# Row counts of direct transfers in a two-layer graph kernel: 128, 32 and 10 rows become 67 and 61, 17 to 31, and 17

## The chip, the cores and the metric

The kernel runs on one core of a Trainium2 chip. The metric is the device time of one execution in microseconds (us). The core has five engines with a queue of instructions each: TensorE (PE; its weight loads are shown as PEld), VectorE (DVE), ScalarE (ACT), GpSimd (POOL) and SyncE (SP). SyncE and ScalarE start direct transfers here, GpSimd starts the gathers, and 16 DMA engines move the bytes of all of them. The names of a queue in the profile end in q where an instruction only starts a transfer (SPq, ACTq, POOLq).

## The reference

Two message-passing layers over a graph with N = 6,250 nodes and E = 200,000 edges, sorted by their target node. A node has 160 numbers: 64 scalars and 32 vectors of three.

```python
# layer one: messages from the source node's row and 4 edge numbers (e0 and the vector e1)
out0 = C0 * (ss * e0 @ W1 + dot * INV3 @ W2)          # ss, vv: rows x[src]
out1 = C1 * (p3 + p4 + p5)                             # products of ss, vv, e0, e1 with W3, W4, W5
m_agg = segment_sum(concat(out0, out1), dst)           # then Ws, Wv, relu, + x
x = layernorm(x + layer_one)
# layer two: weights of the message from 10 edge features
h = relu(edge_length_embedded @ W_fc1 / sqrt(10)) * sqrt(2)
w = h @ W_fc2 / sqrt(100)                              # 192 weights per edge
y = linear(x)[src]
m0, m1, m2, m3 = products of w, y and the 4 edge numbers
out = si(x) + 0.5 * linear(segment_sum(m0..m3, dst))
x = layernorm(x + out)
```

## The kernel before

**Chunks.** The edges are cut into 391 chunks of 512 (128 partitions by J = 4). A written-out order (`ORDER`) mixes the first 312 chunks with the last 79; the last ones have two windows of target nodes each. For every chunk four gathers (`gathered`, L206) fetch the 512 source rows of 640 bytes, from `x` in layer one (`layer = 0` in the code) and from the table `ytab` in layer two. The gathered rows go into a ring of `GRING = 8` chunks.

**Steps.** `sums(layer, ...)` writes one step after another. In step t the chunk at place t of the order is loaded, that of place t - 1 gets its one-hot matrix (`onehot`, VectorE) and in layer two its hidden weights (`hidden`, TensorE L394, in pairs of chunks), place t - 2 its messages (`message`, TensorE L407 and VectorE L410 and L415), place t - 3 its sums on TensorE (`matmuls`, L427), and place t - 4 is added to the running sums (`add`, VectorE). In layer one, where no message is computed, the lags are 0, 1, 2 and 3. Each engine executes its own instructions in the order in which they are written.

**Blocks.** When the last chunk of a block of 128 target nodes is done (`CLOSE[b]`; 49 blocks, the last of 106 rows), the block's own stages follow at fixed lags. In layer one: the node rows are fetched 4 steps after the close (`fetch`, L486), used at lag 8 (`residual`), and the results go to `ytab` and `btab` at lag 14 (`written`, L533 on ScalarE's queue, L537 on SyncE's). In layer two: `btab` is fetched at lag 3 (L486), used at lag 6 (`residual_last`), and the output block is normalized on VectorE and sent at lag 8 (`sent`, L559). Blocks of low node numbers are long: in steps 66 to 200 one closes every 8 steps or so, after that one about every 4.

**The transfers on SyncE's queue.** Besides node rows there are two kinds. Edge attributes (4 numbers per edge, 2,048 bytes per chunk and quarter) come for 32 chunks at a time in four transfers of up to 32 rows into the tile `raw` (L368), asked for 8 steps ahead, and VectorE turns them (L374). Edge features (10 numbers per edge, layer two) come for four chunks at a time, in two transfers of 10 rows with two pieces of 2,048 bytes each (L342; single chunks at the end, L346). They go by turns into the tiles `et` and `early`, are written in the step of their first chunk, and TensorE uses them from the next step on. SyncE executes all of these in the order written, so a transfer that waits for its source or for its tile holds up those behind it.

Of the kernel before, what the change touches and what calls it, by code (L numbers as in the profile page):

```python
# [10 lines left out]
F32 = mybir.dt.float32  # L11
# [7 lines left out]
P = 128  # L19
# [4 lines left out]
J = 4  # L24
CH = P * J
NCH = -(-E // CH)
# [14 lines left out]
HALF = 312  # L41
NWIN = HALF + 2 * (NCH - HALF)
WIDTHS = ((3, 32), (128, 16), (208, 24), (HALF, 32), (NCH, 24))
GRING = 8
PREPARE = 8


def expected(node, sign):
# [30 lines left out]
POS = {c: i for i, c in enumerate(ORDER)}  # L79
# [13 lines left out]
CLOSE = closings()  # L93


def floor_of(c):

    done = [b for b in range(NB) if CLOSE[b] < POS[c]]
    near = [b for b in done if (b >= LATE) == (c >= HALF)] or [b for b in done if b < LATE]
    return P * (max(near) + 1) if near else 0  # L100


def windows(c):
# [108 lines left out]
def windowed(ctx: ExitStack, tc: tile.TileContext, x, srcs, rel, low, ident, iota, early, ahead, ea, sh, avec,  # L212
# [6 lines left out]
    nc = tc.nc  # L219
    const = ctx.enter_context(tc.tile_pool(name="const", bufs=1))  # L220
    dram = ctx.enter_context(tc.tile_pool(name="dram", bufs=1, space=bass.MemoryType.DRAM))
    ytab = dram.tile([N, D], F32, name="ytab")
    btab = dram.tile([N, D], F32, name="btab")

    acc = const.tile([P, 5, NW], F32, name="acc")
    bank = ctx.enter_context(tc.tile_pool(name="bank", bufs=1, space=PSUM)).tile([P, 512], F32, name="bank")
# [13 lines left out]
    def clear(k):  # L240
        nc.scalar.activation(acc[:, k, :], zero[:, 0:1].to_broadcast([P, NW]), AF.Copy)  # L241
# [70 lines left out]
    def sums(layer, table, gp, hp):  # L312
        with ExitStack() as s:
# [11 lines left out]
            G, S, SH, ET, H, M, PA, AT, RAW = {}, {}, {}, {}, {}, {}, {}, {}, {}  # L325

            def load(c):
                if layer or c not in ahead:
                    G[c] = gathered(nc, gp.tile([P, J, D], F32, name="g"), srcs, table, c)
                else:  # L330
                    G[c] = ahead.pop(c)
                if c % 4 == 0 and layer:

                    if POS[c] % 8 >= 4:
                        et = xp.tile([P, 2, CH], F32, name="et")
                    else:
                        et = early.rearrange("p a j d -> p (a j d)")
                        et = et[:, :2 * CH].rearrange("p (s e) -> p s e", s=2)
                    ET[c // 4] = et
                    for i in range(2):  # L340
                        if c + 4 <= NCH:
                            nc.sync.dma_start(et[64 * i:64 * i + 10, :, :],  # L342
                                              ea[:, c * CH:(c + 4) * CH].rearrange("f (s i e) -> f s i e", s=2, i=2)[:, :, i, :])
                        else:
                            for k in range(c + i, NCH, 2):
                                nc.sync.dma_start(et[64 * i:64 * i + 10, (k - c) // 2, :], ea[:, k * CH:(k + 1) * CH])  # L346
# [12 lines left out]
            def group(c):  # L359
                return c - (c - (c >= HALF) * HALF) % 32  # L360

            def attributes(first, n):

                raw = RAW[first] = hp.tile([P, 512], F32, name="raw")
                if n < 32:
                    nc.vector.memset(raw, 0.0)
                for q in range(4):
                    nc.sync.dma_start(raw[32 * q:32 * q + n, :],  # L368
                                      sh[first:first + n, 32 * q:32 * q + 32, :].rearrange("c p f -> c (p f)"))
# [4 lines left out]
                nc.vector.transpose(sht, RAW.pop(first).rearrange("r (p f) -> r f p", f=16))  # L374

            def onehot(c):
                if group(c) == c:
# [6 lines left out]
                attr = SH[group(c)][:, :, c - group(c)].rearrange("p (j k) -> p j k", j=J)  # L384
# [98 lines left out]

            def rows_of(name, table, b):
                t = T[name, b] = np_.tile([P, D], F32, name=name)
                nc.sync.dma_start(t[:rows(b)], table[b * P:b * P + rows(b), :])  # L486

            def fetch(b):
                rows_of("xt", x, b)
# [50 lines left out]
            def fetch_base(b):  # L540
# [15 lines left out]

            def sent(b):
                normed("o", b)
                nc.sync.dma_start(out[b * P:b * P + rows(b), :], T.pop(("o", b))[:rows(b)])  # L559
# [8 lines left out]
            for t in range(max(CLOSE.values()) + 16):  # L568
                for f, lag in stages:
                    if 0 <= t - lag < NCH:  # L570
                        f(ORDER[t - lag])
                for f, lag in reversed(parts):
                    for b in range(NB):
                        if CLOSE[b] == t - lag:
                            f(b)
                if not layer:
                    for k in range(2 * t, min(2 * t + 2, 5)):
                        clear(k)
                if not layer and t == PREPARE:
                    prepare(up, pn)  # L580

# [392 lines left out]
```

## Time and profile before

| | |
|---|---|
| median of 10 runs | 3979.72 us (3978.03 to 3981.49) |
| the profiled execution | 3980.59 us, of which the span from first to last instruction is 3978.4 us |
| TensorE busy, mean granted clock | 3245.4 us (82%), 0.784 |
| VectorE busy | 2189.7 us (55%) |
| GpSimd busy | 2964.8 us (75%) |
| ScalarE busy | 380.5 us (10%) |
| moved by DMA | 295.60 MB, 74 GB/s on average |
| handover from layer one to layer two | GpSimd idle from 1978.3 to 2000.6 us |

A busy share says how much of the span an engine was executing; it is an average over two layers with different loads. The waits say what ended an idle stretch. A group of instructions is named by its line, its engine and output<-inputs. A row of the windows has the stretch, its length, then the busy time and (x) the instructions of TensorE, its weight loads, VectorE, ScalarE and GpSimd, then TensorE's granted clock as a share of full speed, the share of DMA time, and GB/s. A row of the timeline has the start, the duration, the engine, the line, the operation, output<-input, the count, and in brackets the idle time before it and what ended it. The queue rows give packets, megabytes, and the time that the packets took as a share of 16 engines' span.

### The profile page before, as it was taken

The page shows a single profiled execution, that of the slowest core. Times are in us where ns is not written, and L with a number is a line of the kernel's source. Part 1 is how long each engine was busy: PE and PEld are TensorE (multiplying, and loading weights), DVE is VectorE, ACT ScalarE, POOL GpSimd, SP SyncE. Part 2 cuts the span into 40 slices and gives each one's busy share as a digit, 9 for nine tenths or more (in the row PEclk, how much of TensorE's full clock was granted, in tenths as well). Part 3 has the DMA queues.
Part 4 walks back from the last instruction along what each step waited for, and adds up shares of the span by engine and source line. Part 5 has one row for each costly group of instructions (what it writes and reads, how often), then busy time and mean ns, then how long its engine had stood idle before and what let it go on. Part 6 is the DMA issues. An engine that isn't in the chain of part 4 may idle for free.

```text
span 3978.4 us, 42324 instructions
## 1 busy us (share of the span) xinstructions
PE 3245.4 (82%) x12714; PEld 2142.5 (54%) x12715; DVE 2189.7 (55%) x6948; ACT 380.5 (10%) x747; POOL 2964.8 (75%) x3137
## 2 busy tenths in 40 slices
PE   2777777777777777777788998998999999999998
PEld 2444444444444444455555665665666666666665
DVE  4222323233333333344457677777777778788887
ACT  2000000000000000000111111111111111111111
POOL 6777777777777777777667777777777777777775
PEclk8555555565555656666689999999999999999999
DMA  2222222222222222222222222222222222222222
GB/s 76 70 69 66 71 73 68 74 71 75 74 76 73 76 71 78 74 80 79 75 69 73 70 76 73 75 74 74 76 80 76 77 77 77 75 79 77 80 77 67
DMA packets 198245, 295.60 MB, mean 74 GB/s; under 512 B 59270, under 2 KB 140668, under 8 KB 198010
## 3 DMA queue, kind: packets, MB, share of 16 engines
q0 software_dynamic: 150144, 256.45, 24.3%
q1 hardware_dynamic: 40702, 31.55, 2.6%
q10 hardware_dynamic: 7164, 4.80, 0.4%
q8 instruction: 107, 1.75, 0.2%
q14 instruction: 128, 1.05, 0.1%
HBM read 280.57 MB, written 12.00 MB: 74 GB/s over the span
## 4 chain that ended last, share of the span: by engine, by line
POOL 28%; issue 22%; DMA 21%; PE 17%; DVE 11%; ACT 1%; DVEq 0%; POOLq 0%; SPq 0%; ACTq 0%
POOL g L206 28%; DMA g<-in_x,srcs 13%; PE ab L427 10%; DMA g<-ytab,srcs 8%; DVE m L415 3%; PE ph L461 2%; DVE m L410 2%; PE pw L407 2%; DVE S L385 2%; DVE ab L445 1%; DVE ab L444 1%; PE ph L394 1%; PE pl L526 1%; ACT acc L241 1%; DVE bank L381 1%
## 5 line engine op out<-in xcount | busy, mean ns | idle before, releaser
L206 POOL DMA_INDIRECT g<-ytab,srcs x1564 | 1480.0, 946 | 498.5 <-issue 397.9
L206 POOL DMA_INDIRECT g<-in_x,srcs x1556 | 1472.5, 946 | 475.2 <-issue 390.5
L427 PE MATMUL ab<-g,S 128*128 128x160 f32 (+1 forms) x3744 | 1183.5, 495 | 520.6 <-DMA g<-in_x,srcs 405.1
L427 PEld LDWEIGHTS ab<-g,S 128*128 128x128 f32 (+1 forms) x3744 | 727.2, 287 | 984.8 <-DMA g<-in_x,srcs 694.1
L427 PE MATMUL ab<-m,S 128*128 128x320 f32 (+1 forms) x3760 | 966.0, 445 | 14.6 <-DVE acc L449 14.3
L407 PE MATMUL pw<-fc,h 100*128 100x192 f32 x3128 | 660.2, 343 | 145.7 <-DVE m L415 73.3
L427 PEld LDWEIGHTS ab<-m,S 128*128 128x128 f32 (+1 forms) x3760 | 613.8, 193 | 235.3 <-issue 55.5
L447 DVE STREAM_TRANSPOSE ab<-ab 128x160 f32<-128x160 f32 x470 | 170.9, 364 | 1012.9 <-PE ab L427 1012.0
L407 PEld LDWEIGHTS pw<-fc,h 100*128 100x128 f32 x3128 | 501.9, 190 | 414.9 <-issue 298.4
L410 DVE TENSOR_TENSOR m<-pw,g 128x256 f32<-128x256 f32 x782 | 329.3, 421 | 366.1 <-DMA g<-ytab,srcs 313.3
L415 DVE TENSOR_TENSOR m<-g,pw 128x192 f32<-128x192 f32 x1564 | 475.6, 345 | 0.0
L385 DVE TENSOR_TENSOR S<-bank,sh 128x384 f32<-128x384 f32 (+2 forms) x782 | 431.4, 552 | 59.3 <-PE ab L427 9.6
L397 ACT ACTIVATE h<-ph 100x512 f32<-100x512 f32 x391 | 233.4, 597 | 1636.5 <-PE ph L394 1443.1
L449 DVE TENSOR_TENSOR acc<-acc,ab 128x120 f32 (+2 forms) x940 | 261.7, 278 | 186.5 <-PE ph L461 129.6
L381 DVE TENSOR_TENSOR bank<-iota,rel 128x96 f32<-128x96 f32 (+2 forms) x782 | 199.5, 255 | 19.2 <-PE bank L548 18.9
L445 DVE STREAM_TRANSPOSE ab<-ab 32x160 f32<-32x160 f32 x470 | 165.5, 352 | 16.2
L444 DVE STREAM_TRANSPOSE ab<-ab 128x160 f32<-128x160 f32 x470 | 167.4, 356 | 11.1 <-issue 8.2
L461 PE MATMUL ph<-wb,acc 128*128 128x160 f32 (+1 forms) x490 | 135.9, 460 | 0.1
L461 PEld LDWEIGHTS ph<-wb,acc 128*128 128x128 f32 (+1 forms) x490 | 127.9, 325 | 9.1 <-issue 8.7
L394 PE MATMUL ph<-early,fc 10*100 10x512 f32 x392 | 111.8, 633 | 2.2 <-DMA early<-in_ea 2.2
L394 PE MATMUL ph<-et,fc 10*100 10x512 f32 x390 | 109.0, 627 | 2.6 <-DMA et<-in_ea 2.6
L497 ACT ACTIVATE rl<-ph 128x160 f32<-128x160 f32 (+1 forms) x49 | 14.9, 304 | 833.6 <-PE ph L461 833.6
(80 smaller groups left out, 796.9 us busy)
## 6 DMA issues: line engine op xcount, KB each, us to landing
g<-ytab,srcs POOLq DMA_INDIRECT x1564
g<-in_x,srcs POOLq DMA_INDIRECT x1556
raw<-in_sh SPq DMA_DIRECT2D x88, 64.0 KB
early<-in_ea SPq DMA_DIRECT2D x98, 40.0 KB
xt<-in_x SPq DMA_DIRECT2D x48, 80.0 KB
ytab<-y ACTq DMA_DIRECT2D x48, 80.0 KB
btab<-base SPq DMA_DIRECT2D x48, 80.0 KB
et<-in_ea SPq DMA_DIRECT2D x96, 40.0 KB
```

Source lines behind the costliest of these rows:

```text
L206: nc.gpsimd.indirect_dma_start(out=g[:, j, :], out_offset=None, in_=table, in_offset=bass.IndirectOffsetOnAxis(ap=srcs[:, c, j:j + 1], axi ...
L381: nc.vector.tensor_tensor(oh[:, :, :w], iota[:, None, :w].to_broadcast([P, J, w]), rel[:, c, :, None].to_broadcast([P, J, w]), op=ALU.is_e ...
L385: nc.vector.tensor_tensor(S[c][:, :, :, :w], oh[:, :, None, :w].to_broadcast([P, J, 4, w]), attr[:, :, :, None].to_broadcast([P, J, 4, w]) ...
L394: nc.tensor.matmul(ph[:, i, :], fc1[g:g + 10, :], ET[c // 4][g:g + 10, c % 4 // 2, :], start=True, stop=True)
L397: nc.scalar.activation(H[c], H["p"][:, c % 2, :].rearrange("f (p j) -> f j p", j=J), AF.Relu, scale=FC_SCALE)
L407: nc.tensor.matmul(pw[:, j, :], h[:, q + j, :], fc2, start=True, stop=True)
L410: nc.vector.tensor_tensor(mq[:, :, :, 0:64], pw[:, :, 0:128].rearrange("p j (a u) -> p j a u", a=2), y[:, :, None, 0:64].to_broadcast([P, ...
L415: nc.vector.tensor_tensor(mq[:, :, a, 64:160].rearrange("p j (d u) -> p j d u", d=3), y1, pw[:, :, None, w:w + 32].to_broadcast([P, 2, 3, ...
L427: nc.tensor.matmul(ab[:, :n], one[h * i:h * i + h, j, :, :], t[h * i:h * i + h, j, :], start=(j == 0), stop=(j == J - 1), skip_group_check ...
L444: nc.vector.transpose(tr, blocks[:, 1])
L449: nc.vector.tensor_tensor(v, v, tr[:, :, :width(c)], op=ALU.add)
L461: nc.tensor.matmul(po[:r], lhs, weights[:, g, :], start=(g == 0), stop=(g == 4))
```

## The change

Every direct transfer of the running layers is given another row count. The bytes that are computed with stay the same.

- Attributes: the groups of 32 chunks become 15 groups of 31, 23, 19 or 17 chunks (`SIZES`). `group` now returns first chunk and size. The tile is cleared on VectorE before every group; before, only where a group had fewer than 32 chunks.
- Node rows: `fetch`, `fetch_base`, `written` and `sent` go through `sent_rows`, which makes two transfers of 67 and 61 rows out of one of 128. Blocks that close in the last 8 steps, and the block of 106 rows, keep one transfer.
- Edge features: in layer one, at steps 32, 64, ... 256, an eighth of the 10 feature rows is copied into a new table of 17 rows in device memory (`etab`), in one transfer of 10 rows and one that fills rows 10 to 16 with copies of rows 0 to 6. In layer two 17 rows are loaded from it where 10 were loaded from the input. TensorE still reads the first 10.

```diff
+LEADS = 67
+ROWS = 17
+SIZES = (31, 31, 31, 31, 31, 31, 23, 23, 23, 19, 19, 19, 31, 31, 17)
+COPIES = 8
...
+def group(c):
+
+    first = 0
+    for n in SIZES:
+        if c < first + n:
+            return first, n
+        first += n
...
+    etab = dram.tile([ROWS, NCH * CH], F32, name="etab")
...
-                            nc.sync.dma_start(et[64 * i:64 * i + 10, :, :],
-                                              ea[:, c * CH:(c + 4) * CH].rearrange("f (s i e) -> f s i e", s=2, i=2)[:, :, i, :])
+                            nc.sync.dma_start(et[64 * i:64 * i + ROWS, :, :],
+                                              etab[:, c * CH:(c + 4) * CH].rearrange("f (s i e) -> f s i e", s=2, i=2)[:, :, i, :])
...
-            GROUPS = sorted(((a, min(32, end - a)) for begin, end in ((0, HALF), (HALF, NCH))
-                             for a in range(begin, end, 32)), key=lambda g: POS[g[0]])
+            GROUPS = sorted({group(c) for c in range(NCH)}, key=lambda g: POS[g[0]])
...
-                if n < 32:
-                    nc.vector.memset(raw, 0.0)
+                nc.vector.memset(raw, 0.0)
...
+            def sent_rows(engine, b, to, from_):
+
+                cut = LEADS if CLOSE[b] < NCH - 8 and rows(b) == P else rows(b)
+                for part in (slice(0, cut), slice(cut, rows(b))):
+                    if part.start < part.stop:
+                        engine.dma_start(to[part], from_[part])
...
-                nc.sync.dma_start(t[:rows(b)], table[b * P:b * P + rows(b), :])
+                sent_rows(nc.sync, b, t, table[b * P:b * P + rows(b), :])
...
-                nc.scalar.dma_start(ytab[b * P:b * P + r, :], y[:r])
+                sent_rows(nc.scalar, b, ytab[b * P:b * P + r, :], y)
...
-                nc.sync.dma_start(btab[b * P:b * P + r, :], base[:r])
+                sent_rows(nc.sync, b, btab[b * P:b * P + r, :], base)
...
-                nc.sync.dma_start(out[b * P:b * P + rows(b), :], T.pop(("o", b))[:rows(b)])
+                sent_rows(nc.sync, b, out[b * P:b * P + rows(b), :], T.pop(("o", b)))
...
+                if not layer and t >= 2 * PREPARE and t % 32 == 0 and t // 32 <= COPIES:
+
+                    part = slice((t // 32 - 1) * (NCH * CH // COPIES), t // 32 * (NCH * CH // COPIES))
+                    nc.sync.dma_start(etab[0:10, part], ea[:, part])
+                    nc.sync.dma_start(etab[10:ROWS, part], ea[0:ROWS - 10, part])
```

More of the change, by code (lines that the diff above doesn't have):

```diff
@@ L341, in load @@
                         if c + 4 <= NCH:
-                            nc.sync.dma_start(et[64 * i:64 * i + 10, :, :],
-                                              ea[:, c * CH:(c + 4) * CH].rearrange("f (s i e) -> f s i e", s=2, i=2)[:, :, i, :])
+                            nc.sync.dma_start(et[64 * i:64 * i + ROWS, :, :],
+                                              etab[:, c * CH:(c + 4) * CH].rearrange("f (s i e) -> f s i e", s=2, i=2)[:, :, i, :])
                         else:
                             for k in range(c + i, NCH, 2):
-                                nc.sync.dma_start(et[64 * i:64 * i + 10, (k - c) // 2, :], ea[:, k * CH:(k + 1) * CH])
+                                nc.sync.dma_start(et[64 * i:64 * i + ROWS, (k - c) // 2, :], etab[:, k * CH:(k + 1) * CH])
                 for first, n in GROUPS:
@@ L357, in sums @@
                 last = POS[first]
-            def group(c):
-                return c - (c - (c >= HALF) * HALF) % 32
             def attributes(first, n):
                 raw = RAW[first] = hp.tile([P, 512], F32, name="raw")
-                if n < 32:
-                    nc.vector.memset(raw, 0.0)
+                nc.vector.memset(raw, 0.0)
                 for q in range(4):
@@ L376, in onehot @@
             def onehot(c):
-                if group(c) == c:
+                first = group(c)[0]
+                if first == c:
                     turn(c)
@@ L383, in onehot @@
                 S[c] = ring[:, POS[c] % 3]
-                attr = SH[group(c)][:, :, c - group(c)].rearrange("p (j k) -> p j k", j=J)
+                attr = SH[first][:, :, c - first].rearrange("p (j k) -> p j k", j=J)
                 nc.vector.tensor_tensor(S[c][:, :, :, :w], oh[:, :, None, :w].to_broadcast([P, J, 4, w]),
```

## The prediction

> **What bounds the kernel now.** I read the page first (shares, slices, costliest groups), then GpSimd's timeline, the windows of layer two, and the SyncE queue's timeline beside TensorE's.
>
> ```profile
> span 3978.4 us, 42324 instructions
> PE 3245.4 (82%) x12714; PEld 2142.5 (54%) x12715; DVE 2189.7 (55%) x6948; ACT 380.5 (10%) x747; POOL 2964.8 (75%) x3137
> ...
> q1 hardware_dynamic: 40702, 31.55, 2.6%
> q10 hardware_dynamic: 7164, 4.80, 0.4%
> ...
> L206 POOL DMA_INDIRECT g<-ytab,srcs x1564 | 1480.0, 946 | 498.5 <-issue 397.9
> L206 POOL DMA_INDIRECT g<-in_x,srcs x1556 | 1472.5, 946 | 475.2 <-issue 390.5
> ```
>
> GpSimd issues 3,128 gathers, 946 ns each and 0.30 us between two, so 1.25 us per gather and 5.0 us per chunk of four. 3,128 x 1.25 is 3,910 of the 3,978 us. Its waits are only these 0.30 us gaps; the rest is the start and the 22 us between the layers. So GpSimd is the clock, and another engine costs time only where it can't do a chunk in 5.0 us. In layer two (from 2,000 us) TensorE is near that:
>
> ```profile
> 2000.00:2370.00 370.00, 332.64 (x1432) 220.88 (x1433) 255.82 (x843) 44.97 (x76) 279.49 (x296) 0.97 0.27 73
> 2370.00:2970.00 600.00, 544.01 (x2424) 364.27 (x2424) 438.28 (x1440) 74.58 (x132) 453.76 (x481) 0.99 0.28 76
> 2970.00:3978.00 1008.00, 932.12 (x4304) 643.01 (x4302) 800.30 (x2512) 126.73 (x233) 746.80 (x789) 0.98 0.28 76
> ```
>
> The second number is the stretch, the third TensorE's busy time: idle 56 us from 2,370 to 2,970 and 76 us from 2,970 on, which is all that can pay back a delay there. What can delay TensorE is seen in these lines, SyncE's queue and then TensorE:
>
> ```profile
> 3494.28 0.37 SPq L559 DMA_DIRECT2D out<-z  x1
> 3494.81 0.66 SPq L342 DMA_DIRECT2D et<-in_ea  x2
> 3495.51 0.35 SPq L486 DMA_DIRECT2D base<-btab  x1
> 3495.97 0.68 SPq L342 DMA_DIRECT2D early<-in_ea  x2
> 3496.70 1.71 SPq L368 DMA_DIRECT2D raw<-in_sh  x4
> ```
>
> ```profile
> 3497.51 1.21 PE L394 MATMUL ph<-et,fc 10*100 10x512 f32 x4 [0.54 <-DMA et<-in_ea]
> ```
>
> SyncE waits in order for VectorE's output block (L559), and the edge features of the next four chunks (L342) stand behind it. They are issued at 3,494.81 and used at 3,497.51: a lead of 2.7 us, of which TensorE waited 0.54. So a load takes 2.2 to 2.9 us today and in places has nothing to spare.
>
> **How many DMA engines a transfer gets.** The trace has no prime row count, but it counts completion packets of 4 bytes, one per DMA engine used. SyncE's queue has 7,200 of them, and that is exactly the sum over its 531 transfers of the largest divisor of the row count that is at most 16: 16 for 128, 64 or 32 rows, 12 for 24, 15 for 15, 10 for 10 or 100, 2 for 106. By this, 17, 19, 23, 31, 61 and 67 rows get one engine. The packets of the 106-row transfers run as two chains of 53, the next 640-byte packet 28 ns after the last, so an engine drains one packet after another. I take one engine, the same one each time, for every changed transfer.
>
> The Trainium skill, "DMA: Bandwidth & Descriptors", section "Why a DMA increments its semaphore by 16 and not by 1", speaks against this change: the engine count is the largest k up to 16 that divides the slowest dimension of both sides, and 127 partitions get 1. The nearest row, 106 rows on two engines, would halve the terms below and give no slowdown; by the rule it is the sum below. No run shown here has a prime count.
>
> **Prices on one engine.** 128 rows of 640 bytes: 128 x 28 ns = 3.6 us (67 and 61 rows queue behind each other). Edge features of four chunks: 2 transfers x 17 rows x 2 packets of 2,048 bytes, 68 x 80 ns (from a packet's start to the completion packet behind it) = 5.4 us, where 10 rows on ten engines had 4 packets per engine, 0.3 us. Attributes of 31 chunks: 4 x 31 x 80 ns = 9.9 us, against 0.6. The engine also serves 1/16 of each gather, some 0.24 us in 1.25, so the prices are divided by 0.81: 4.4, 6.7 and 12.2 us. The page's queue lines give 19 bytes per ns for an engine (31.55 MB in 2.6% of 16 spans): 4.3, 7.3 and 13.4 us, near enough.
>
> **Edge features, layer two (on the path).** Behind an output block, a load lands 0.5 us (the output was issued earlier) before 2.2 + 4.4 + 6.7 us, so 12.9 us after issue. Bounds: 11.2 with no gather on the engine (2.2 + 3.6 + 5.4), 18 with a base block's 4.4 us and part of another in front too. I take 12.9, since the base fetch mostly follows. I listed issue and first use of the 96 loads after the first two. First used from 2,370 to 2,970: 10 have a lead below 12.9, short by 48 us together, 6 by more than 3.4. After 2,970: 28, short by 190 us, 25 by more than 3.4. (At 11.2: 34 and 143 us; at 18: 100 and 346.) Node blocks close every 8 steps early and every 4 late, hence the difference. TensorE runs in order, so a late load stops it, and VectorE, the output block and SyncE behind it; the next lead is no longer for that.
>
> **Attributes.** Each load now begins with a VectorE clear at its step (485 ns, 30 of them for 4), and SyncE is held until VectorE is there. Behind wait the next edge features: 12 to 13 us of attributes + 7 + 2, about 23 us from that step. The first use follows 2 to 5 steps later, by the group list. Two steps (10 us) are short by 13, three by 8, four by 3: 29 us for the groups at steps 105, 167 and 179, 32 for 218, 249, 303 and 326. (Bounds: 15 and 12 us at undisturbed prices; the same again if a block stands in front.) The attributes themselves are asked for 9 steps ahead, 45 us, and are in time. Four more transposes (1.04 us) and the clears lie in VectorE's idle 45%.
>
> **The clock.** After the 6.05 us idle between the layers, TensorE's granted clock is 0.50 from 2,002 to 2,013.4: the same work took some 5.7 us more. A short dip at 2,235 made 14 matmuls take 4.02 us instead of about 2.3, 1.5 us more. The granted clock changes in steps of 3.4 us in this trace, so I count stalls over 3.4 us; each leaves a full queue of work behind, and I take 2.5 us for one, nearer the short dip: 15 us early, 62 late (bounds 1.5 and 5.7).
>
> The Trainium skill, "TensorE: Matmul & The Clock Gate", section "Part 1: The HAM clock gate", has half rate after an idle window of about 3.4 us and full rate after one busy window. That would be 1.7 us a stall, an estimate from that page, and 25 us less in the sum.
>
> **At nothing.** Layer one: node rows are fetched 4 steps (20 us) before use, against some 15 us for three 128-row moves; a group of attributes in front makes a block 8 us late, hidden by TensorE's idle quarter and the gather ring of 8 chunks, 40 us (13 x 8 = 104 us without it). The 16 copies into the padded table move 100,096 bytes per row, 5.3 us on up to ten engines, twice per step 32 to 256: a gather 11 us late, hidden by the ring (85 us without). The first attributes land at about 48 us instead of 34; the sums wait for ScalarE's clear until 61. ScalarE and SyncE issue 0.35 us for each added transfer, both idle. The last 8 steps' blocks are not split, so the handover and the end keep theirs, give or take 5 us. Gathers wait for a 2,048-byte packet before each of their own, under 0.3 us, and GpSimd waits for none of them.
>
> **Sum.** 2,370 to 2,970: 48 + 29 + 15 - 56 idle = 36 us. After: 190 + 32 + 62 - 76 = 208. Together 244 on the profiled 3,980.6 us (span 3,978.4; the median of the runs is 0.9 us lower): 4,225 us.
>
> **Rivals.**
> - *The rows spread over two engines or more.* Then a load behind a block lands after 2.2 + 11.1 / 2 - 0.4 = 7.4 us. Up to about 8.5 us the shortfall (75 us late, 17 early) is within the idle time: 3,981 us, not slower. For it: no prime in the trace; against it: the 7,200 completion packets.
> - *The one engine is itself the bound.* After 2,970 it has 48 edge sets (139 KB), 67 node blocks (82 KB) and 1.2 MB of attributes: 13.3 MB, 702 us at 19 bytes per ns in 1,008. It binds from 13.2 down; at 10 it needs 1,334 us, and with the early part that is about 4,430. Against it: 28 ns packets on a two-engine transfer.
> - *Loads overtake.* If output blocks and base fetches do not hold the features up, a load lands after 2.2 + 6.7 = 8.9, with the attributes' share some 10 us: 112 - 76 late, cold starts 1.5 x 14: about 4,040.
>
> **How the numbers follow.** 0.72 for the forecast (its own range 4,090, from the low bounds 143 + 12 + 32 - 76, to 4,400), 0.08 for several engines, 0.12 for the saturated engine, 0.08 for the small case. The range 4,060 to 4,440 leaves out the several engines and the outer ends of the others. Above 0.2% (8 us, about what can be told from no change) slower: 0.91; the same 0.07; faster 0.02, since nothing is taken from GpSimd.
>
> **What would show it.** Right: TensorE waits at L394 for the features some 40 times, up to 10 us, mostly after 2,970; the clock there falls below 0.98; GpSimd shows waits for VectorE's messages late in layer two; layer one ends within 10 us of 2,000; the SyncE queue's completion packets fall to one per changed transfer. Wrong: no L394 wait above 3 us (several engines), or layer one longer by more than 20 us (copies or node rows not hidden).

## The result and the profile after

The changed kernel takes 4278.94 us (median of 8 runs, 4273.41 to 4283.25) against 3980.00 us (28 runs of the kernel before beside it): a ratio of 1.0751 (95% interval 1.0741 to 1.0760), 299 us slower. The forecast was 4,225 us with a range of 4,060 to 4,440. The profiled execution took 4273.03 us, of which the span is 4271.2. In the changed kernel the lines have moved: `gathered` is L220, the features are loaded at L357 and used at L405, the attributes are loaded at L378, all split node rows are sent at L472, the copies are at L600 and L601.

The page of the changed kernel, the lines that answer to those shown of before, with the clock slices and the two feature groups:

```profile
span 4271.2 us, 42714 instructions
PE 3273.1 (77%) x12714; PEld 2229.2 (52%) x12715; DVE 2190.7 (51%) x6978; ACT 379.2 (9%) x747; POOL 2967.5 (69%) x3137
...
PEclk8555555555565666667899999998998889887898
...
q1 hardware_dynamic: 37994, 50.75, 3.5%
...
L220 POOL DMA_INDIRECT g<-ytab,srcs x1564 | 1482.0, 948 | 725.2 <-issue 437.9
L220 POOL DMA_INDIRECT g<-in_x,srcs x1556 | 1473.2, 947 | 489.7 <-issue 401.5
...
L405 PE MATMUL ph<-early,fc 10*100 10x512 f32 x392 | 166.3, 715 | 129.9 <-DMA early<-etab 129.7
L405 PE MATMUL ph<-et,fc 10*100 10x512 f32 x390 | 163.2, 706 | 116.7 <-DMA et<-etab 116.7
```

The two feature groups of before:

```profile
L394 PE MATMUL ph<-early,fc 10*100 10x512 f32 x392 | 111.8, 633 | 2.2 <-DMA early<-in_ea 2.2
L394 PE MATMUL ph<-et,fc 10*100 10x512 f32 x390 | 109.0, 627 | 2.6 <-DMA et<-in_ea 2.6
```

Over the whole span no engine works noticeably more: GpSimd's gathers still take 948 ns each. What has grown is GpSimd's idle time before the gathers of layer two, from 498.5 to 725.2 us, and TensorE now waits 246.4 us for edge features, where it waited 4.8. Of the 4-byte completion packets on SyncE's queue 1,483 are left where there were 7,200. That is exactly the forecast's sum over all transfers, in which each one of 17, 19, 23, 31, 61 or 67 rows counts one.

Where the 293 us of the span went is read from the times at which gathers are issued. The columns are: last gather of layer one; from there to the first gather of layer two; from the first to the last gather of layer two; from the last gather to the end.

| kernel | layer one | handover | layer two | end | span |
|---|---|---|---|---|---|
| before | 1977.4 | 23.3 | 1955.3 | 22.5 | 3978.4 |
| after | 1992.6 | 32.8 | 2174.3 | 71.5 | 4271.2 |
| difference | +15.2 | +9.5 | +219.0 | +49.0 | +292.8 |

Layer two can be set against the terms of the sum with two windows over the same steps (72 to 200 and 200 to 388, from TensorE's first use of the features loaded in one step to that of the other), first of before, then of after. The second stretch is the one in which node blocks close every four steps.

```profile
2356.80:2998.20 641.40, 583.47 (x2619) 391.58 (x2618) 471.59 (x1547) 79.54 (x140) 485.12 (x513) 0.99 0.28 75
2998.20:3941.90 943.70, 878.20 (x4020) 605.61 (x4019) 751.23 (x2353) 120.99 (x221) 713.94 (x755) 0.99 0.29 77
```

```profile
2390.80:3071.10 680.30, 608.31 (x2619) 420.24 (x2618) 467.76 (x1550) 79.28 (x140) 501.63 (x531) 0.91 0.27 76
3071.10:4229.60 1158.50, 988.96 (x4020) 675.43 (x4019) 751.53 (x2366) 120.27 (x221) 703.57 (x743) 0.86 0.23 65
```

The same 4,020 matmuls take 988.96 us of TensorE instead of 878.20, at a mean granted clock of 0.86 instead of 0.99, and the stretch is 214.8 us longer; the earlier stretch is 38.9 us longer. What TensorE waits for in the late stretch, after (line, what it waited for, us in total, times, longest):

```profile
PE ph L405 <- DMA et<-etab: 84.5, 30, 6.5
PE ph L405 <- DMA early<-etab: 83.8, 28, 10.5
PE ab L438 <- DVE acc L460: 0.9, 3, 0.4
```

There are 168.3 us of waits for features, and hardly any other wait is left. GpSimd's longest total waits for another engine over the whole kernel, after:

```profile
POOL g L220 <- DVE bank L392: 121.4, 52, 9.5
...
POOL g L220 <- DVE m L426: 101.6, 48, 11.2
```

GpSimd, which had only its 0.30 us gaps and the handover before, now waits up to 11 us for VectorE's one-hot matrices and messages, and these follow TensorE.

One load shows the mechanism. SyncE's timeline of after, then TensorE's (start, duration, engine, line, operation, in brackets the idle time before it):

```profile
3587.61 0.80 SPq L472 DMA_DIRECT2D out<-z  x2
3588.50 1.44 SPq L357 DMA_DIRECT2D et<-etab  x2
```

```profile
3583.06 1.10 PE L405 MATMUL ph<-early,fc 10*100 10x512 f32 x4
...
3590.31 2.32 PE L438 MATMUL ab<-m,S 128*128 128x320 f32 x8
3597.86 2.00 PE L405 MATMUL ph<-et,fc 10*100 10x512 f32 x2 [5.24 <-DMA et<-etab]
3601.05 2.02 PE L405 MATMUL ph<-et,fc 10*100 10x512 f32 x2 [1.20 <-DMA et<-etab]
3603.01 2.93 PE L418 MATMUL pw<-fc,h 100*128 100x192 f32 x8
3605.73 3.35 PE L438 MATMUL ab<-m,S 128*128 128x320 f32 x8
3608.91 1.47 PE L418 MATMUL pw<-fc,h 100*128 100x192 f32 x8
```

The output block's two transfers go first, the features stand behind them. The packets of SyncE's queue in the trace have the same order: the block's 640-byte packets run from 3,588.38 to 3,593.76 us, the features' 2,048-byte packets start at 3,593.77, and the completion packets of their two transfers come at 3,597.15 and 3,600.41. The first transfer can be used 9.4 us after issue, the second 12.55 us after issue; TensorE waits for both, 6.4 us together. After the first wait it works at half the clock (granted 0.5 from 3,597.6 to 3,607.8): the four L405 matmuls take 4.02 us instead of 1.10, eight of L418 2.93 instead of 1.47, eight of L438 3.35 instead of 2.32. That is another 5.4 us, until 3,608.9. A load was waited for at its first use 41 times in layer two, 29 of them in the late stretch.

### The profile page after: what moved, and what is told of

Read it like the earlier page. It is cut to its first block, busy times and chain, and to the rows that moved or that the text cites. A ratio compares the mean times of both kernels' runs of the same rounds, so it can differ in the third digit from the quotient of the medians.

```text
span 4271.2 us, 42714 instructions
## 1 busy us (share of the span) xinstructions
PE 3273.1 (77%) x12714; PEld 2229.2 (52%) x12715; DVE 2190.7 (51%) x6978; ACT 379.2 (9%) x747; POOL 2967.5 (69%) x3137
## 4 chain that ended last, share of the span: by engine, by line
PE 39%; DMA 30%; POOL 16%; issue 11%; DVE 3%; ACT 1%; SPq 1%; DVEq 0%; ACTq 0%; POOLq 0%
PE ab L438 20%; POOL g L220 16%; DMA g<-in_x,srcs 16%; PE pw L418 11%; DMA et<-etab 7%; DMA early<-etab 6%; PE ph L405 5%; DMA g<-ytab,srcs 1%; PE ph L479 1%; PE bank L566 1%; DVE m L426 1%; ACT acc L256 1%; PE pl L544 1%; PE pl L543 1%; DVE m L421 0%
## 5 line engine op out<-in xcount | busy, mean ns | idle before, releaser
L220 POOL DMA_INDIRECT g<-ytab,srcs x1564 | 1482.0, 948 | 725.2 <-issue 437.9
L220 POOL DMA_INDIRECT g<-in_x,srcs x1556 | 1473.2, 947 | 489.7 <-issue 401.5
L438 PE MATMUL ab<-g,S 128*128 128x160 f32 (+1 forms) x3744 | 1078.9, 474 | 642.7 <-DMA g<-in_x,srcs 567.9
L438 PEld LDWEIGHTS ab<-g,S 128*128 128x128 f32 (+1 forms) x3744 | 713.2, 284 | 1014.8 <-DMA g<-in_x,srcs 694.6
L438 PE MATMUL ab<-m,S 128*128 128x320 f32 (+1 forms) x3760 | 1002.1, 463 | 4.2 <-DVE acc L460 4.0
L438 PEld LDWEIGHTS ab<-m,S 128*128 128x128 f32 (+1 forms) x3760 | 644.0, 204 | 237.5 <-issue 74.4
L418 PEld LDWEIGHTS pw<-fc,h 100*128 100x128 f32 x3128 | 563.3, 207 | 267.4 <-issue 228.6
L418 PE MATMUL pw<-fc,h 100*128 100x192 f32 x3128 | 667.1, 360 | 36.9 <-DVE m L426 14.8
L405 PE MATMUL ph<-early,fc 10*100 10x512 f32 x392 | 166.3, 715 | 129.9 <-DMA early<-etab 129.7
L405 PE MATMUL ph<-et,fc 10*100 10x512 f32 x390 | 163.2, 706 | 116.7 <-DMA et<-etab 116.7
L405 PEld LDWEIGHTS ph<-early,fc 10*100 10x100 f32 x392 | 36.2, 177 | 201.1 <-issue 136.8
L405 PEld LDWEIGHTS ph<-et,fc 10*100 10x100 f32 x390 | 35.6, 175 | 186.8 <-issue 120.0
L479 PE MATMUL ph<-wb,acc 128*128 128x160 f32 (+1 forms) x490 | 124.8, 431 | 0.1
```

What stands on the lines that cost most here:

```text
L220: nc.gpsimd.indirect_dma_start(out=g[:, j, :], out_offset=None, in_=table, in_offset=bass.IndirectOffsetOnAxis(ap=srcs[:, c, j:j + 1], axi ...
L405: nc.tensor.matmul(ph[:, i, :], fc1[g:g + 10, :], ET[c // 4][g:g + 10, c % 4 // 2, :], start=True, stop=True)
L418: nc.tensor.matmul(pw[:, j, :], h[:, q + j, :], fc2, start=True, stop=True)
L438: nc.tensor.matmul(ab[:, :n], one[h * i:h * i + h, j, :, :], t[h * i:h * i + h, j, :], start=(j == 0), stop=(j == J - 1), skip_group_check ...
```

## The experiments

In the expectations A is the forecast's theory: transfers of a prime row count lie on one DMA engine, feature loads come in behind an output block, TensorE stalls and goes cold. B and C are its rivals: in B the one engine is the bound by its load, whichever transfer that comes from; in C SyncE is held up by the clears and the doubled transfers. Eight kernels ran on chips where the kernel before took 3979.9 us (13 runs, the first four of them) and 3980.5 us (19 runs, the next four). Their account, in the columns of the table above:

| kernel | layer one | handover | layer two | end | span |
|---|---|---|---|---|---|
| features_only | 1982.3 | 23.3 | 1956.6 | 54.0 | 4016.3 |
| nodes_only | 1979.3 | 32.2 | 1956.8 | 34.6 | 4003.0 |
| attributes_only | 1979.0 | 23.3 | 1958.2 | 25.3 | 3985.8 |
| features_early | 1994.6 | 32.3 | 1956.1 | 25.1 | 4008.1 |
| features_16 | 1993.8 | 32.7 | 1957.5 | 41.2 | 4025.1 |
| features_10 | 1979.0 | 32.7 | 1956.9 | 35.0 | 4003.6 |
| copies_only | 1982.4 | 23.4 | 1954.8 | 24.6 | 3985.2 |
| copies_small | 1978.3 | 23.3 | 1954.7 | 24.6 | 3980.9 |

**One part alone: features.** Node rows and attributes as before; the copies and the 17-row loads stay.

```diff
-LEADS = 67
-SIZES = (31, 31, 31, 31, 31, 31, 23, 23, 23, 19, 19, 19, 31, 31, 17)
+LEADS = 128
+SIZES = (32,) * 9 + (24, 32, 32, 15)
```

> Only the edge features are changed: the copies into the padded table and the loads of 17 rows on one engine. Attributes and node rows are as before, on 16 engines. Theory A (a load behind an output block comes too late for TensorE, because both stand one behind the other on one DMA engine): without the 4.4 us of the block the second of the two feature transfers lands 2.2 + 6.7 = 8.9 us after issue, so by the list of leads 85 us are short from 2,998 us on and 19 before, a dozen late cold starts at the 3.8 us that the changed kernel showed each, minus 76 and 56 us of idle time: some 55 us in layer two, plus 15 us that GpSimd lost beside the copies in layer one. 4,030 to 4,070 us. Theory B (the load of one engine, whichever transfer it comes from, slows the gathers): features are half the packets' time on that engine, so about half of the 299 us, 4,120 to 4,150. Theory C (SyncE is held by clears and by twice as many transfers): neither is there, 3,980 to 4,000.

Measured 4019.51 us (4017.29 to 4025.80), ratio 1.0103 (1.0086 to 1.0120): 40 us, under the low end expected. TensorE waits 60 us for features, never more than 3.4 us at once; the second transfers that it waited for could be used 8.2 to 9.5 us after issue, where the expectation had 8.9. In the table GpSimd's layer two is only 1.3 us longer; TensorE only ends 32 us later behind the last gather. So the features alone are late, but the ring of gathered chunks takes up the lag.

**One part alone: node rows.** 67 and 61 rows; features in 10 rows from the input, no copies, old attribute groups.

```diff
-SIZES = (31, 31, 31, 31, 31, 31, 23, 23, 23, 19, 19, 19, 31, 31, 17)
+SIZES = (32,) * 9 + (24, 32, 32, 15)
-    nc.sync.dma_start(et[64 * i:64 * i + ROWS, :, :], etab[:, ...])
+    nc.sync.dma_start(et[64 * i:64 * i + 10, :, :], ea[:, ...])
-    (the copies into etab)
```

> Only the node rows are changed, 67 and 61 rows; features are 10 rows from the input, no copies, attributes as before. Theory A: a feature load waits behind 4.4 us of an output block on the one engine, and lands 6.5 us after issue; some 35 us short in the second half of layer two against 76 us idle, so nothing there. What is left is the handover, 10 us longer in the changed kernel: 3,980 to 3,995 us. Theory B: about 40% of the 299 us, 4,080 to 4,110. Theory C (twice as many transfers on SyncE): 4,000 to 4,050.

Measured 4002.99 us (3997.21 to 4006.76), ratio 1.0054 (1.0038 to 1.0071): 23 us, above what was expected. The waits of nodes_only that name the places:

```profile
PE ph L406 <- DMA early<-in_ea: 29.8, 11, 8.0
...
PE ph L406 <- DMA et<-in_ea: 20.6, 8, 4.0
...
DVE base L554 <- DMA btab<-base: 7.8, 2, 4.0
```

The features have their ten engines here and are late all the same, 50 us together, since the one engine that serves the node rows stands in their way; that is nearly all hidden. What shows are 9 us in the handover and 12 us at the end.

**One part alone: attributes.** Only the groups of 31 to 17 chunks and the clears.

```diff
-LEADS = 67
+LEADS = 128
-    nc.sync.dma_start(et[64 * i:64 * i + ROWS, :, :], etab[:, ...])
+    nc.sync.dma_start(et[64 * i:64 * i + 10, :, :], ea[:, ...])
-    (the copies into etab)
```

> Only the attributes are changed: 15 groups, a clear before each, 31 to 17 rows on one engine. Theory A: features behind them are late at seven places by 13 us at most, between which TensorE's idle time makes it good: 3,980 to 3,990 us. Theory B: 10% of the 299 us, 4,000 to 4,020. Theory C (SyncE held by VectorE's clear): 4,000 to 4,080, with waits of TensorE at L405 after every group.

Measured 3987.20 us (3985.78 to 3988.44), ratio 1.0018 (1.0009 to 1.0028), as expected: 7 us.

The three parts alone cost 40, 23 and 7 us: 70 of the 299.

**The features asked for four steps earlier.** Everything of the change stays; each feature load is written at the first chunk of the set before it, so it has some 20 us more.

```diff
+    for p in ((0, 4) if POS[c] == 0 else (POS[c] + 4,)):
+        if p < NCH:
+            features(ORDER[p])
```

> The changed kernel with every transfer as it is, the same rows, engine and queue, but each feature load is written four steps earlier, as soon as its tile is free. Theory A: the lead behind an output block grows from 3 to 10 us to 20 us and more, the load takes 12.5 us, and TensorE's waits for features go from 246 us to under 30. GpSimd is the clock again in layer two: 4,005 to 4,040 us, the rest being layer one's 15 us beside the copies, 10 us at the handover and the start of layer two. Theory B (the engine's load): nothing is taken from it, 4,230 to 4,290. Theory C (SyncE held): the clears and the doubled transfers are still there, 4,150 to 4,290.

Measured 4011.27 us (4009.97 to 4012.18), ratio 1.0079 (1.0062 to 1.0096), as expected by A. Page of features_early (the last two columns are the mean ns of one and the idle time before them):

```profile
L409 PE MATMUL ph<-early,fc 10*100 10x512 f32 x392 | 110.8, 636 | 0.0
L409 PE MATMUL ph<-et,fc 10*100 10x512 f32 x390 | 109.8, 636 | 0.0
```

The waits for features are gone, 246.4 us to 0.0, and with them 268 of the 299 us. The bytes, the row counts and the one engine are the same, so the engine's load as such can't have been the bound. What is left, 31 us, is mostly layer one (17 us) and the handover (9 us) by the table. This run shows that the time is lost because the loads come late; the next one shows that they come late by their row count.

**Features in 16 rows.** Everything else as in the change.

```diff
-ROWS = 17
+ROWS = 16
```

> The changed kernel with 16 rows of features in place of 17: the padded table, the copies, the clears and the split node rows stay, and the bytes of a load go down by 6%. Theory A: a load is spread over 16 engines, 4 or 5 packets on each, and on the first engine it stands behind 4.4 us of an output block: it lands 6.5 us after issue, TensorE's waits for features fall from 246 to under 60 us and lie within the idle time: 4,000 to 4,040 us. If bytes and copies mattered and not the engine count: 4,250 to 4,280. Theory C (SyncE held): 4,200 to 4,280.

Measured 4028.35 us (4025.73 to 4031.22), ratio 1.0121 (1.0104 to 1.0138), as expected. Page of features_16:

```profile
L405 PE MATMUL ph<-early,fc 10*100 10x512 f32 x392 | 117.7, 658 | 33.5 <-DMA early<-etab 33.5
L405 PE MATMUL ph<-et,fc 10*100 10x512 f32 x390 | 113.3, 643 | 26.1 <-DMA et<-etab 26.1
```

One row less takes the feature waits from 246.4 to 59.6 us and 251 us off the time. The padded table, the copies and the number of transfers are as before it, so it is the row count that makes the features late; the 59.6 us that remain are about what nodes_only has too (50 us).

**Node rows and attributes without the features.**

```diff
-    nc.sync.dma_start(et[64 * i:64 * i + ROWS, :, :], etab[:, ...])
+    nc.sync.dma_start(et[64 * i:64 * i + 10, :, :], ea[:, ...])
-    (the copies into etab)
```

> The changed kernel without the padded table: features are 10 rows from the input again, no copies; node rows and attributes stay changed. Theory A: as with 16 rows, but without the 15 us that GpSimd lost beside the copies in layer one: 3,985 to 4,020 us. Theory C (SyncE held): 4,180 to 4,270.

Measured 4005.78 us (4005.39 to 4011.90), ratio 1.0068 (1.0051 to 1.0085), as expected. Node rows and attributes together cost 25 us, about the sum of each alone (30), and the features on top of them cost 273. Only all of it together is more than the ring can hide.

**The copies alone, and the copies in small pieces.** copies_only is the kernel before plus the 16 copies; copies_small makes the same bytes in one chunk's columns per step.

```diff
-    if not layer and t >= 2 * PREPARE and t % 32 == 0 and t // 32 <= COPIES:
-        part = slice((t // 32 - 1) * (NCH * CH // COPIES), t // 32 * (NCH * CH // COPIES))
+    if not layer and t < NCH:
+        part = slice(t * CH, (t + 1) * CH)
```

> The kernel before with the 16 copies into the padded table added, which nothing reads. The record said that the ring of 8 chunks hides them: 3,980 to 3,983 us. The trace of the changed kernel says otherwise: GpSimd never had more than 8 gathers in flight, and while packets of 50,048 bytes of 1.85 us each stood between a gather's packets, it waited for the oldest to land, 15.4 us in all: 3,992 to 3,999 us.

> The same copies in 391 pieces of 512 columns, two at each step of layer one, so that the packets are of 2,048 bytes; nothing reads the table. The same bytes move. If it is the size of the packets that holds the gathers up: 3,978 to 3,984 us. If it is the bytes, 3,992 to 3,999. If SyncE's extra 782 instructions hold up node rows, more than 4,000.

copies_only: 3986.30 us (3985.43 to 3988.01), ratio 1.0015 (1.0005 to 1.0024). That is 5.8 us, between the two expectations, so neither was met. copies_small: 3981.11 us (3980.49 to 3984.42), ratio 1.0003 (0.9993 to 1.0012), as expected: no cost that can be told from none. GpSimd's waits for earlier gathers, in copies_only and then in copies_small:

```profile
POOL g L220 <- DMA g<-in_x,srcs: 18.0, 41, 3.1
```

```profile
POOL g L220 <- DMA g<-in_x,srcs: 7.3, 24, 0.3
```

The same bytes in small pieces leave only the usual 0.30 us gaps; in eighths of a row GpSimd waits up to 3.1 us for gathers. The kernel before has the same gaps as copies_small:

```profile
POOL g L206 <- DMA g<-in_x,srcs: 7.9, 26, 0.3
```

The other ten of the 15 us in layer one appear only where the node rows lie on the one engine too (features_early and features_16: 16 to 17 us; nodes_only: 2).

The mechanism is seen in the profile of the change. SyncE's queue, GpSimd and TensorE at the first copies:

```profile
147.36 3.46 SPq L600 DMA_DIRECT2D etab<-in_ea  x1
150.86 0.77 SPq L601 DMA_DIRECT2D etab<-in_ea  x1
151.68 0.77 SPq L600 DMA_DIRECT2D etab<-in_ea  x1
152.49 0.81 SPq L601 DMA_DIRECT2D etab<-in_ea  x1
```

```profile
151.28 0.94 POOL L220 DMA_INDIRECT g<-in_x,srcs  x1 [0.30 <-issue]
152.53 0.95 POOL L220 DMA_INDIRECT g<-in_x,srcs  x1 [0.30 <-issue]
...
160.04 0.95 POOL L220 DMA_INDIRECT g<-in_x,srcs  x1 [0.30 <-issue]
161.95 0.94 POOL L220 DMA_INDIRECT g<-in_x,srcs  x1 [0.97 <-DMA g<-in_x,srcs]
166.36 0.94 POOL L220 DMA_INDIRECT g<-in_x,srcs  x1 [3.47 <-DMA g<-in_x,srcs]
```

```profile
161.74 0.91 PE L438 MATMUL ab<-g,S 64*128 64x160 f32 x4 [3.05 <-DMA g<-in_x,srcs]
165.73 0.99 PE L438 MATMUL ab<-g,S 64*128 64x160 f32 x4 [3.09 <-DMA g<-in_x,srcs]
```

The sums at 161.74 and 165.73 wait for the gathers issued at 151.28 and 152.53. The gather at 161.95 is the eighth after the one of 151.28, and goes out only when that has landed; the next in the same way. The trace shows why it is the eighth: the gathers count their landings on eight semaphores in turn (103 to 110), in before as in after, and each waits until the gather that used its semaphore last has landed. So eight gathers are in flight at most, 10 us of them, and the ring of eight chunks (32 gathers) is no cover against a gather that lands late. That it lands late because of the copies is shown by copies_only and copies_small; in the trace their rows travel in packets of 50,048 bytes, 1.86 us each in the median and 3.5 at most, four copies at once.

**Four kernels on another chip.** Their kernel before took 4925.1 us (18 runs, 4910 to 4940), 945 us more than on the others. GpSimd is not held to 1.25 us per gather there but waits for other engines' signals. From the waits of nodes_base4:

```profile
POOL g L220 <- DVE bank L393: 413.3, 102, 9.1
...
POOL g L220 <- remote: 267.6, 96, 6.5
```

TensorE is idle more of the time there (61% busy in features_18, against 82% in before on the others), so a late load can cost less. The expected times were made for 3,980 us and can't be tested on it; the four kernels are compared with one another and with the kernel before on that chip. Between runs of one kernel the times spread there by 22 to 31 us.

*features_18*, the change with 18 rows:

```diff
-ROWS = 17
+ROWS = 18
```

> The changed kernel with 18 rows of features in place of 17: one row more, so 6% more bytes per load and copies of 10 and 8 rows; clears and split node rows stay. If the engine count follows from the largest divisor up to 16, 18 rows go to 9 engines with 4 packets each per transfer, and the load lands some 7 us after issue behind an output block on the first engine: 4,020 to 4,045 us, and the completion packets of the 197 loads rise from 1 to 9 each. If a row count that is no multiple of 16, or not 10, were the trouble: 4,250 to 4,300.

Measured 4934.91 us (4922.43 to 4948.08), ratio 1.0019 (1.0003 to 1.0034). The time is 10 us above before, and 38 us below nodes_64, where the features have 17 rows on one engine while the node rows have sixteen; as the two kernels differ in both, this is not the price of the row count alone. What does not hang on the time is the count of completion packets on SyncE's queue: 3,067, by the sum exactly 9 for each 18-row transfer, where 17 rows had 1.

*nodes_64*, the change with node rows as 64 and 64:

```diff
-LEADS = 67
+LEADS = 64
```

> The changed kernel with node rows split as 64 and 64 in place of 67 and 61: as many transfers and the same bytes, but 16 engines. Features (17 rows) and attributes stay on one engine. Theory A: without the block's 4.4 us in front a feature load lands 8.9 us after issue, as in the kernel with the features alone changed; with the attributes' share and no handover loss 4,020 to 4,050 us. Theory C (SyncE held by twice as many transfers): 4,200 to 4,280.

Measured 4972.64 us (4964.04 to 4986.55), ratio 1.0106 (1.0073 to 1.0139), 48 us above before. Layer two takes 2582.1 us in its profile, against 2554.8 in features_18. As a ratio this is where A would lie (4,020 us is 1.010 of 3,980) and far from C (4,200 is 1.055), but on this chip it remains a hint.

*nodes_base4*, nodes_only with four buffers for `base` (the expectation speaks of `y` too, but `y` kept two):

```diff
-base = np_.tile([P, D], F32, name="base")
+base = np_.tile([P, D], F32, name="base", bufs=4)
```

> The kernel with only the node rows changed, and four buffers in place of two for the tiles base and y, from which the rows are written at the end of layer one. In the trace of the kernel with the node rows alone VectorE waited 3.99 and 3.82 us there for the write of the block two before (L554), and ScalarE 2.10 and 1.63 us. If these waits make the handover longer (32.2 us from last to first gather, against 23.3): 24 to 28 us there, and 3,993 to 3,999 us in place of 4,003. If it is the late fetch of the last block's rows: no change from 4,003.

Measured 4940.27 us (4924.13 to 4950.15), ratio 1.0030 (1.0013 to 1.0047). VectorE's wait for `base` to come free is gone, but the handover takes 50.2 us here against 48.6 in features_18, 43.3 in nodes_64 and 46.9 in all_hidden. Whether four buffers return the 9 us stays open.

*all_hidden*, features_early with the small copies and four buffers for `base` (again `base` alone):

```diff
+features(ORDER[p])              # four steps earlier, as above
+part = slice(t * CH, (t + 1) * CH)
+base = np_.tile([P, D], F32, name="base", bufs=4)
```

> The changed kernel with the same prime row counts on the same engine, and every wait that was found given room: features asked for four steps earlier, copies in pieces of 512 columns, four buffers for base and y. If the account is complete, the 299 us go to within 5 to 20 us: 3,985 to 4,000. If one engine's load itself costs something that the earlier runs did not show: over 4,010.

Measured 4979.53 us (4970.74 to 5001.39), ratio 1.0127 (1.0091 to 1.0162). That is 54 us above before, the slowest of the four, so the expectation was not met: 4,010 us, its mark for a cost that the account lacks, is 1.0075 of 3,980. The waits for features are gone here too (0.0 us), and layer two takes 2556.2 us, as in features_18. What is longer is layer one: 2308.9 us against 2267.2 in features_18, 2274.8 in nodes_64 and 2268.1 in nodes_base4, and the only change in layer one that none of those has is the copies in small pieces. So on this chip, beside the split node rows, the small pieces seem to cost some 34 to 42 us, where copies_small had no cost; this rests on one profile of each kernel, and why was not found. That the last 31 us are the copies and the handover is therefore read from traces, not shown by taking them away. No kernel here is faster than the one before; on the chips with 3,980 us, GpSimd's 1.25 us per gather sets the floor.

## Why the prediction was right

**One DMA engine.** Right. The trace of before had no prime row count, only the 7,200 completion packets as a sum of divisors; after, the same rule gives 1,483 exactly, 3,067 for 18 rows, 4,430 for 16 rows, and 16 rows take away three quarters of the feature waits. The Trainium skill, "DMA: Bandwidth & Descriptors", section "Why a DMA increments its semaphore by 16 and not by 1", states this rule, and every count of these runs agrees with it. The rival with several engines has gone: its sign was no wait over 3 us at the features' use, and the longest is 10.5.

**The landing time.** The forecast took 12.9 us behind an output block (bounds 11.2 and 18). In the load shown the second transfer can be used after 12.55: 6.65 us for the features' own packets (6.7 in the forecast) and 5.9 for the block and the rest (2.2 + 4.4 - 0.5 = 6.1). But the forecast set this time against the first use, and TensorE begins with the first transfer, which is there after 9.4 us (9.0 to 9.6 in most loads behind an output block). The waits are so split in two: 175 us for the first transfers of the 41 late sets, 71 for the second.

**The sum of layer two.** Predicted 36 and 208 us, measured 38.9 and 214.8 over nearly the same stretches. The terms are less good than the sum:

| term | early: predicted, measured | late: predicted, measured |
|---|---|---|
| waits for features, behind blocks and attributes | 77, 69 | 222, 164 |
| cold clock (more TensorE time for the same matmuls) | 15, 25 | 62, 111 |
| idle time that pays back | -56, -55 | -76, -60 |
| sum | 36, 39 | 208, 215 |

The measured waits are those after less those before (0.5 and 4.3 us). Two terms were mis-sized, in opposite directions: 66 us too much waiting and 59 us too little cold clock over both stretches. That they cancel to within 10 us, together with the idle time, is luck.
- *The shortfall after 2,970* was put at 190 + 32 and is 164. Of the 32 for attributes 11 came: the load at step 252 behind an attribute group was not waited for at all, the one at 220 for 2.2 us at its second transfer alone, those at 304 and 328 for 4.9 and 4.1 us. That leaves some 153 of the 190 behind blocks; there the first transfer comes some 3 us sooner than the 12.9 that were taken. That fits a TensorE which is by then far enough behind that the next features, issued with the group, still land in time; it was not tested. The early attribute term was good: 5.4, 9.7 and 8.6 us at steps 108, 168 and 180, 24 against the 29 predicted, and 27 with their second transfers; those features were used 22, 17 and 18 us after the attributes' issue, against some 23.
- *The cold clock* was put at 2.5 us for each stall over 3.4 us, 25 of them late. It is 3.8 us for each of the 29 late loads (111 / 29). The step took the price from a short dip. The load shown above costs 5.4: the second wait comes while TensorE is still cold, so half rate holds for 10 to 11 us. Over layer two from 2,380 us on, 27 of the 44 stretches at clock 0.5 last 10.2 or 13.7 us; in nodes_only, where a late load is one wait, and a shorter one, 26 of 30 last 3.4 or 6.8. The Trainium skill, "TensorE: Matmul & The Clock Gate", section "Part 1: The HAM clock gate", has full rate after at least one busy window; with one, the forecast's estimate from that page was 1.7 us a stall. These runs show more than twice that for a load. That a load here is two waits fits this, but the second wait was not tested apart from the longer first one.

**What was put at nothing.** Four steps failed.
- *The copies: "a gather 11 us late, hidden by the ring".* The gathers were late, and the ring did not hide it, since only eight are in flight. Layer one's last gather is 15.2 us later.
- *The handover, "give or take 5 us".* It is 9.5 us longer. The last blocks keep one transfer, as the forecast said, but those before them do not, and they still hold the engine. VectorE in the handover, after:

```profile
2008.99 0.38 DVE L553 SCALAR_TENSOR_TENSOR base<-pl,a_sb,z 128x160 f32<-128x160 f32 x1 [3.93 <-DMA btab<-base]
2011.78 0.33 DVE L521 SCALAR_TENSOR_TENSOR z<-xt,rl 106x160 f32<-106x160 f32 x1 [2.41 <-DMA xt<-in_x]
...
2017.45 0.38 DVE L553 SCALAR_TENSOR_TENSOR base<-pl,a_sb,z 128x160 f32<-128x160 f32 x1 [3.84 <-DMA btab<-base]
```

  `base` has two buffers, so block b waits until the write of block b - 2 has left the one engine, twice 3.9 us, and the last `xt` comes 2.4 us late. How the 9.5 us divide between them was not separated.
- *The start of layer two.* From its first gather to step 72 the change takes 365.4 us instead of 356.2. The forecast had no term before 2,370. One load there, at step 28 behind an attribute group, was waited for 3.1 us at its first use and 1.2 at its second transfer, and the one at step 68, also behind a group, 2.5 us at its second; the rest of the 9 us was not taken apart.
- *The end, put at give or take 5 us:* 5.1 us from step 388 on, at the edge of what was allowed.

Together these are 15.2 + 9.5 + 9.2 + 5.1 = 39 us, and they and the 10 us by which the layer-two sum was short are the whole distance of 49 us between the 244 us predicted and the 293 us of the profile. The median is 6 us above the profiled execution.

**What the forecast named as signs.** The waits for features (41 sets, up to 10.5 us), the clock below 0.98 (0.91 and 0.86), GpSimd waiting for VectorE's messages late in layer two, and the completion packets came as named. "Layer one ends within 10 us of 2,000" did not: it ends at 2,025, 24.8 us later than before. That is past the mark of 20 us which the forecast set as a sign of copies or node rows that are not hidden, and it was right about that.

**The rivals.** The saturated engine is excluded by features_early, which moves the same bytes over the same engine in 268 us less. SyncE held up (C) is excluded by features_16, with the same number of transfers and the same clears in 4028 us, where C had 4,200 or more. Loads did not overtake: the late ones up to step 384 were first used 9.0 us after issue or later, when only half of the set was there, and the set of the load shown was complete at 12.55, against the rival's 8.9.

## What to carry to other kernels

Before changing a tile's row count, count the completion packets of its transfers: they give the number of DMA engines per transfer, and one row more can turn sixteen engines into one, while everything that is queued behind it on that engine is late too. A late load costs its wait and the cold matmuls after it, and it shows in the time only once the buffers between the engines are used up; parts that cost 7, 23 and 40 us alone came to 299 together. Asking for the load one set earlier took back 268 of them without a change in the transfer.

## What the runs showed of the hardware that was not expected

- In these kernels at most eight gathers are in flight. The ninth is issued when the first has landed (161.95 after 161.74, 166.36 after 165.73), whatever room the ring of destination tiles has, because the gathers share eight semaphores in turn. That is how the program is built; whether the chip has a limit of its own no run here shows.
- Long rows copied from device memory to device memory go in packets of 50,048 bytes that take 1.85 to 3.51 us; the same bytes in pieces of one chunk's columns cost nothing that could be measured where the node rows were whole (3981.1 us against 3986.3, and 3980.5 without copies). all_hidden, with split node rows and on another chip, had a longer layer one with the pieces.
- SyncE's issue of a transfer, 0.35 us before, itself stalls when much is outstanding. SyncE's queue of after:

```profile
3647.02 0.69 SPq L472 DMA_DIRECT2D out<-z  x2
3647.80 1.51 SPq L357 DMA_DIRECT2D et<-etab  x2
3649.35 7.47 SPq L472 DMA_DIRECT2D base<-btab  x2
```

  Two issues take 7.47 us behind four transfers on the one engine. What room is full there the trace does not say.
- One chip ran the unchanged kernel in 4925 us instead of 3980, with the waits at signals between engines. Why was not found.
